# Second half's row variances moved from VectorE to ScalarE in a cross-attention and gated FFN kernel, with three groups of sums replanned

## The chip, the cores and the metric

The kernel runs on one core of one Trainium2 chip. The metric is device time in microseconds (us) of one execution; the median of three runs before the change is 1160.4 (1158.4 to 1164.2). Engines are called as in the profile: PE is TensorE (matmuls and transposes), PEld its weight loads, DVE is VectorE, ACT is ScalarE, POOL is GpSimd, and SP is SyncE, which here only issues DMAs.

## The reference

Everything is float32. `x` and `ctx` are 16 sequences of 128 tokens of 1024 numbers.

```python
def _layernorm(x, axis=-1, eps=1e-05):
    m = jnp.mean(x, axis=axis, keepdims=True)
    v = jnp.var(x, axis=axis, keepdims=True)
    return (x - m) / jnp.sqrt(v + eps)
...
query = q @ w_q.T          # q = _layernorm(x); 32 heads of 32
key = k @ w_k.T            # k = v = ctx; 8 groups of 32
value = v @ w_v.T
scores = jnp.einsum('bghnd,bgsd->bghns', query, key) / D_HEAD ** 0.5
scores = jnp.where(mask, scores, jnp.finfo(scores.dtype).min)
attention = jax.nn.softmax(scores, axis=-1)
out = jnp.einsum('bghns,bgsd->bghnd', attention, value)
...
x = x + out @ w_out.T
x12 = jnp.einsum('bsk,mk->bsm', _layernorm(x), w12) + b12
x1, x2 = jnp.split(x12, 2, axis=-1)
x = x + jnp.einsum('bsm,nm->bsn', jax.nn.silu(x1) * x2, w3) + b3
```

The first layernorm is what the change concerns. Its mean is taken out of the weights of the query product ahead of time (`centre`, L442), so that the product runs on the raw `x`. Its standard deviation comes in later: the scores are multiplied by the row's 1/std when they are masked (L760). So the variance of a token is needed only once attention reaches that token's sequence.

## The kernel before, in words

**Halves.** The 2048 tokens are two halves T = 0 and 1 of eight sequences (`NT` = 8). Sequence t belongs to half t // 8. The tile `mr[T]` holds two numbers for each token of a half: in row 0 the mean (or minus it), in row 1 the variance, which `inv_std` (L213) turns into 1/std with five small POOL instructions and two of ACT (Ln, Exp).

**Products by seven.** Large matrix products are not done with eight block products but with seven, as in Strassen's method: sums and differences of blocks of the left and right operand are made first ("left sums", "right sums"), and each product's result is added into several outputs. `seven` (L272) runs one such group; the order of the seven products is a tuple like (1, 5, 6, 7, 2, 3, 4). In the query stage a product is four matmuls of 512 columns, and steps 0 to 9 take them in the order (1, 5, 6, 7, 2, 3, 4). After each product it calls `hook(j)`, j = 1 to 7, through which all other work is placed.

**The query stage.** The query product uses seven twice, one inside the other. The outer level has products 1 to 7 ("outer 7"), the inner level too. A *step* is one outer product for one half g of the output rows: `Q_STEPS` has 14 of them, outer 1, 2, 6, 7, 4, 5, 3 in this order, each for g = 0 and 1. So steps 6 and 7 are outer 7, and steps 12 and 13 are outer 3. Each step has seven inner products of its own, and four sums of right-hand blocks (inner sums 5, 6, 7, 4 in the code's numbering) that both steps of an outer product share. `q_outer_right` (L488) makes the outer blocks, most of them on POOL; `q_inner_right` (L501) makes the inner sums, all on DVE.

The plan is written by hand: `q_at(n, j, fn, ...)` (L472) puts a call at hook j of step n, and `q_plans` (L633) holds the table. In the tables `((5, 2), (5, 7), (6, 1), (6, 2))` for outer 7 means: inner sum 5 is issued at hook 2 of step 5, sum 6 at hook 7 of step 5, sum 7 at hook 1 of step 6, sum 4 at hook 2 of step 6. Calls at one place run in the order in which they were registered.

**Order of instructions.** PE follows the source order throughout, and DVE from the start to the end of the first half's attention. In steps 0 to 9 (`AHEAD` = 10) ACT, POOL and SP follow it too. Elsewhere a scheduler orders ACT, POOL and SP by priority and by when memory is free. An engine waits at the head of its own queue: what stands behind a waiting instruction waits as well.

**Memory.** Nearly all operands of 128 x 1024 live in one pool of `NUNIT` = 44 units, 4 KB for each partition. A load or a sum that needs a new unit waits until one has had its last reader. PSUM has eight banks.

**Variances.** For the first half, tile t (128 tokens x 1024) is loaded by SP at hook 1 of step t + 1 (`load_xs`, L416), and `q_squares` (L622) runs at hook 2 of step t + 2, on ACT: one pass that sums the row, one tiny instruction that makes it minus the mean, and one pass that sums the squares of the centred row. For the second half, the loads are issued in the keys' and values' second round (`seven_round(1, k)`, L716; hooks 1 to 4 of each k), and `q_stats` (L617) runs at hooks 3 to 6: `mean_var` (L205), that is two BATCH_NORM_STATS2, an aggregate and a copy on DVE. The last one is followed by `inv_std`.

**After step 9.** Attention of the first half begins. It is cut into 16 units (a sequence and half of its heads); PE's other work is cut into the units by a cost: steps 10 to 13, then the rounds (1, 0) and (1, 1) for the second half's keys and values, then the first round of the output product. A unit takes DVE four times an instruction that scales and masks the scores (`s`, L760) and a row maximum (`nmax`, L763); ACT takes the exponentials (`p`, L769); DVE inverts the sums (`inv`, L778); POOL multiplies (`p`, L781); PE transposes (`pt`, L788); DVE and ACT copy the result out of PSUM (`pT`, L791 and L793); and PE multiplies by the values (`o`, L803). In the rounds (1, k) DVE and POOL also make the right sums of the context (`ctx_T`, `ctx`, L700) and of the output weights (`wo_T`, `wo`, L242), and POOL makes the left sums of the keys' weights (`sums_left7`, tile `A_S`, L303).

Of the kernel before, what the change touches and what calls it, by code (L numbers as in the profile page):

```python
# [13 lines left out]
AF = mybir.ActivationFunctionType  # L14
ALU = mybir.AluOpType
# [5 lines left out]
D = 1024  # L21
# [10 lines left out]
NT = B // 2  # L32
# [96 lines left out]
def xattn_ffn_kernel(  # L129
# [33 lines left out]
    nc = tc.nc  # L163
# [11 lines left out]
    def temp(shape, name):  # L175
        return temps.tile([P, *shape], F32, tag="tmp", name=name)
# [14 lines left out]
    def load(src, shape, name, eng=nc.sync):  # L191
        t = unit(shape, name)
        eng.dma_start(t, src)
        return t
# [10 lines left out]
    def mean_var(xt, dst, name):  # L205
        st = small.tile([P, 2, nc.vector.BN_STATS_DIM], F32, tag="st", name=f"st_{name}")
        for h in range(2):
            nc.vector.bn_stats(st[:, h, :], xt[:, ts(h, 512)])  # L208
        mv = small.tile([P, 2], F32, tag="mv", name=f"mv_{name}")
        nc.vector.bn_aggr(mv, st)  # L210
        nc.vector.tensor_copy(dst, mv)

    def inv_std(mr, name):  # L213

        n = mr.shape[2]
        v, t = (small.tile([P, NT], F32, tag=f"inv_std{i}", name=f"is{i}_{name}", bufs=2)[:, :n] for i in range(2))
        y = mr[:, 1, :]
        nc.gpsimd.tensor_scalar(v, y, EPS, None, ALU.add)
        nc.scalar.activation(t, v, AF.Ln)
        nc.scalar.activation(y, t, AF.Exp, scale=-0.5)  # L220
        nc.gpsimd.tensor_mul(t, y, y)
        nc.gpsimd.tensor_mul(t, t, v)
        nc.gpsimd.tensor_scalar(t, t, -0.5, 1.5, ALU.mult, ALU.add)
        nc.gpsimd.tensor_mul(y, y, t)
# [177 lines left out]
    mr = [const.tile([P, 2, NT], F32, tag=f"mr{T}", name=f"mr_{T}") for T in range(2)]  # L402
    later, xs = [], {}

    def soon(n, gen):

        later.append([n, gen])

    def tick():
        for item in list(later):  # L410
            item[0] -= 1
            if item[0] <= 0:
                later.remove(item)
                stream.work.appendleft(item[1])

    def load_xs(t):  # L416
        xs[t] = load(x[t], [D], f"xs_{t}")

    def stats(t):
        mean_var(xs.pop(t), mr[t // NT][:, :, t % NT], f"a{t}")  # L420

    def turn_V(T, c, r, t):

        pt = bank(f"vt_{T}_{c}_{r}").rearrange("p (t k) -> p t k", t=4)
        for i in range(4):
            nc.tensor.transpose(pt[:, i, :], t[:, ts(i, S)], ident)
            yield 0.17
        if (T, c) not in V:
            V[T, c] = unit([4, KV], f"V_{T}_{c}")
        nc.scalar.copy(V[T, c][:, :, ts(r, P)], pt)  # L430

    def key_home(T, c, r):
        if (T, c) not in KT:
            KT[T, c] = unit([GH, 512], f"K_{T}_{c}")
        return KT[T, c][:, r, :]
# [36 lines left out]
    def q_at(n, j, fn, *args):  # L472
        qplan.setdefault((n, j), []).append((fn, args))
# [140 lines left out]
            *((INNER,) if n < AHEAD else ((1, 6, 5, 7, 2, 3, 4), nc.vector.tensor_copy)),  # L614
        )

    def q_stats(t):  # L617
        stats(t)
        if t % NT == NT - 1:
            inv_std(mr[t // NT], f"a{t // NT}")  # L620

    def q_squares(t):  # L622

        xt = xs.pop(t)
        less = mr[0][:, 0, t : t + 1]
        nc.scalar.activation(xt, xt, AF.Identity, accum_out=less)
        nc.scalar.mul(less, less, -1.0 / D)
        nc.scalar.activation(xt, xt, AF.Square, bias=less, accum_out=mr[0][:, 1, t : t + 1])
        if t == NT - 1:
            nc.gpsimd.tensor_scalar(mr[0][:, 1, :], mr[0][:, 1, :], 1.0 / D, None, ALU.mult)  # L630
            inv_std(mr[0], "a0")

    def q_plans():  # L633
        for n, (g, i) in enumerate(Q_STEPS):
            if i > 2:
                q_at(n - 2, 3, q_load_left, g, i)
            for e, k in enumerate((1, 5, 6, 7, 3)):
                q_at(n - 1, 3 + e if n else min(5 + e // 2, 7), q_inner_left, g, i, k)
            if i in (1, 2, 5, 3):
                q_at(n - 1, 6 if n else 7, q_hold, g, i)  # L640
            if i == 1:
                q_at(g - 1, 7, q_keep_left, g, 4)
                q_at(g - 1, 7, q_outer_left, g)
                q_at(g, 7, q_keep_left, g, 3, 6)
                q_at(g + 1, 2, q_keep_left, g, 5, 7)
                q_at(n + 1, 2, q_store, g, i, "U")
            if i == 2:
                q_at(n + 1, 2, q_gather, g, 2, "U")
                q_at(n + 2, 3, q_final, g, 2, 0, 0)
            if i == 6:  # L650
                q_at(n - 2, 4, q_fetch, g, "U")
                q_at(n + 1, 2, q_store, g, "u", "V")
            if i == 7:
                q_at(n + 1, 2, q_store, g, "u", "W")
            if i == 4:
                q_at(n, 7, q_stay, g, "u", 1)
            if i == 5:
                q_at(n + 1, 3, q_gather, g, "V", 5)
                q_at(n + 1, 3, q_gather, g, "W", 5)
                q_at(n + 1, 4, q_given, g, "W", 1)  # L660
            if i == 3:
                q_at(*((n + 1, 3) if g == 0 else (n, 7)), q_gather, g, "V", 3)
                q_at(n, 7, q_given, g, "V", 0)
        for e, (K, C) in enumerate(((0, 0), (1, 0), (1, 1), (0, 1))):
            for f, (h, c) in enumerate(((0, 0), (0, 1), (1, 1), (1, 0))):
                when = ((-1, 3 + (f + 1) // 2), (0, 1 + f), (0, 5 + f // 2), (1, 2 + f))[e]
                q_at(*when, load_xq, K, C, h, c)
        for i, hcs, ks in (
            (1, [(-1, 5)] * 4, ((-1, 6), (-1, 6), (-1, 7), (0, 1))),
            (2, [(0, 6)] * 4, ((0, 7), (1, 1), (1, 2), (1, 7))),  # L670
            (5, [(2, 1), (2, 2), (2, 7), (3, 1)], ((8, 7), (9, 1), (9, 2), (9, 7))),
            (6, [(2, 7), (3, 1), (3, 3), (3, 3)], ((3, 5), (3, 6), (3, 7), (4, 1))),
            (7, [(4, 5), (5, 1), (5, 2), (5, 5)], ((5, 2), (5, 7), (6, 1), (6, 2))),
            (4, [(6, 5), (7, 1), (7, 2), (7, 5)], ((7, 2), (7, 7), (8, 1), (8, 2))),
            (3, [(4, 4)] * 4, ((4, 4), (5, 4), (8, 4), (8, 6))),
        ):
            for when, hc in zip(hcs, ((0, 0), (0, 1), (1, 1), (1, 0))):
                q_at(*when, q_outer_right, i, *hc)
            for when, k in zip(ks, (5, 6, 7, 4)):
                q_at(*when, q_inner_right, i, k)  # L680
        for t in range(NT):
            q_at(t + 1, 1, load_xs, t)
            q_at(t + 2, 2, q_squares, t)
        for m in (0, 1, 4, 5):
            q_at(8, 1 + m, q_home, 0, m)
        q_at(11, 3, load_left7, 1)
        for j, e in ((1, 0), (1, 5), (2, 1), (4, 3)):
            q_at(12, j, lambda e=e: ctx_work[1][e][1]())
        for when, i, e in (
            ((12, 6), 5, 0), ((12, 7), 5, 1), ((13, 2), 6, 0), ((13, 4), 6, 1), ((13, 5), 7, 0), ((13, 7), 7, 1),  # L690
        ):
            q_at(*when, ctx_sum, i, e)
        q_at(13, 3, sums_left7, 1, 0)

    def ctx_sum(i, e):

        R, (a, b) = ctx_R[1], {5: (0, 1), 6: (3, 5), 7: (3, 0), 4: (2, 6)}[i]
        if e == 0:
            R[i] = R[0] if i == 7 else [unit([2, 512], f"ctx_1_T{i}_{h}") for h in range(2)]
        (nc.vector if i in (5, 6) else nc.gpsimd).tensor_sub(R[i][e], R[a][e], R[b][e])  # L700
# [15 lines left out]
    def seven_round(T, k, R):  # L716
        def done(rc, s, ps):
            r, c = rc
            dst = temp([512], f"vT_{T}_{c}_{r}") if k else key_home(T, c, r)
            if s is None:  # L720
                nc.scalar.copy(dst, ps)
            else:
                nc.vector.tensor_add(dst, s, ps)
            if k:
                soon(3, turn_V(T, c, r, dst))

        def hook(j):
            tick()
            if (T, k, j) == (1, 0, 4):
                sums_left7(1, 1)  # L730
            if (T, k) == (1, 0) and j < 3:
                ctx_sum(4, j - 1)
            if T == 1 and j < 5:
                load_xs(NT + 4 * k + j - 1)
            if T == 1 and j > 2 and j < 7:
                q_stats(NT + 4 * k + j - 3)
            transition(T, k, j)

        yield from seven(left7.pop((T, k)), R, f"Q7_{T}_{k}", done, hook, (1, 2, 5, 6, 7, 3, 4))
# [616 lines left out]
    for t in range(8, B):  # L1356
        n, j = divmod(t - 8, 2)
# [68 lines left out]
```

## Time and profile before

| | us |
|---|---|
| median of three runs (lowest, highest) | 1160.4 (1158.4, 1164.2) |
| the profiled execution | 1160.87 |
| its span, first to last instruction | 1159.1 |

| stage (us from the span's start) | length | PE | DVE | ACT | POOL |
|---|---|---|---|---|---|
| first keys and values, 0 to 57.7 | 57.7 | 55.9 | 27.8 | 12.5 | 33.2 |
| query steps 0 to 9, 57.7 to 181.3 | 123.6 | 121.6 | 103.3 | 31.8 | 89.5 |
| first half's attention, 181.3 to 356 | 174.7 | 166.9 | 146.7 | 105.5 | 111.6 |
| second half's attention and output product, 356 to 600 | 244.0 | 242.3 | 177.7 | 153.0 | 141.0 |
| rest of it and FFN's first product, 600 to 976 | 376.0 | 374.8 | 255.2 | 61.3 | 167.0 |
| FFN's second product, 976 to 1159.1 | 183.1 | 179.0 | 138.7 | 31.5 | 103.5 |

The columns under the engines are busy time in us. A line of the timeline gives the start, the duration, the engine, the source line, the operation and its operands as "output <- inputs", and in brackets the idle time before it with what ended it. The name of a tile is without its number: `Y_T` is an inner right sum of the query stage, `xq` a block of `x`, `Q_b` a PSUM bank of a query step (the keys' and values' rounds use the same name), `QI` an inner left sum, `QL` a left operand fetched again, `xs` a tile of `x` for the variances, `st_a` the statistics of DVE.

Steps 0 to 9 begin at 57.7, 71.0, 83.0, 95.0, 107.0, 119.0, 131.1, 145.3, 157.3 and 169.3, so a step takes 12.0, but for step 0 (13.3) and step 6 (14.2). Steps 10 to 13, between units of attention, begin at 182.5, 196.8, 214.0 and 233.5; the round (1, 0) begins at 258.7.

### The profile page before, as it was taken

What the parts mean: (1) busy time and instruction counts of PE and PEld (TensorE: products, weight loads), DVE (VectorE), ACT (ScalarE), POOL (GpSimd) and SP (SyncE); (2) the same over time, 40 slices, a digit from 0 to 9 for tenths busy, and PEclk for the clock granted to TensorE, in tenths of its full rate; (3) what the DMA queues carried; (4) which work ended last, traced back from release to release, by engine and by line L of the source; (5) the groups of instructions that cost most, each with busy time, mean ns of one, the idle gap of its engine ahead of it and who ended that gap; (6) DMA issues with size and microseconds to landing.
All of it is one profiled execution on the core that took longest, in us unless ns stands there. A gap on an engine that the chain in (4) does not pass through costs nothing.

```text
span 1159.1 us, 13631 instructions
## 1 busy us (share of the span) xinstructions
PE 1140.4 (98%) x4232; PEld 533.0 (46%) x4232; DVE 849.4 (73%) x1179; ACT 395.6 (34%) x1429; POOL 645.7 (56%) x591
## 2 busy tenths in 40 slices
PE   9999999989999999999999999999999999999998
PEld 4444444544544455444454544444444444444443
DVE  4577988798897778778545456757777887979872
ACT  1222234556666576676361321110011022111211
POOL 5669935776468556646533359822523342548455
PEclk9999999999999999999999999999999999999999
DMA  9699675955344330332584889758734878272411
GB/s 365 254 372 346 223 267 150 214 134 180 110 164 183 128 128 37 128 128 110 182 308 163 333 327 327 228 199 264 171 130 157 214 192 270 91 268 86 172 74 72
DMA packets 70232, 227.42 MB, mean 196 GB/s; under 512 B 7824, under 2 KB 7824, under 8 KB 70160
## 3 DMA queue, kind: packets, MB, share of 16 engines
q1 hardware_dynamic: 62672, 199.81, 46.4%
q0 software_dynamic: 6624, 24.12, 11.2%
q10 hardware_dynamic: 864, 2.62, 0.6%
q8 instruction: 34, 0.56, 0.2%
q14 instruction: 38, 0.31, 0.1%
HBM read 139.49 MB, written 79.69 MB: 189 GB/s over the span
## 4 chain that ended last, share of the span: by engine, by line
PE 70%; DVE 4%; ACT 1%; issue 1%; POOL 1%; DMA 0%; SPq 0%; POOLq 0%; DVEq 0%; ACTq 0%
PE F_b L199 28%; PE G_b L199 15%; PE O_b L199 15%; PE pt L788 3%; PE Q_b L199 3%; PE s L751 2%; PE o L803 2%; DVE s L760 1%; PE xt L903 1%; DVE nmax L763 1%; ACT p L769 0%; DMA xnr<-xn_dram 0%; POOL p L781 0%; DVE xnT L1079 0%; DVE st_a L208 0%
## 5 line engine op out<-in xcount | busy, mean ns | idle before, releaser
L769 ACT ACTIVATE p<-s,nmax 128x128 f32<-128x128 f32 x512 | 181.5, 402 | 117.7 <-DVE nmax L763 102.8
L781 POOL TENSOR_TENSOR p<-p,inv 128x512 f32<-128x512 f32 x128 | 132.2, 1067 | 124.9 <-DVE inv L778 105.2
L199 PE MATMUL F_b<-X_T,L 128*128 128x512 f32 x304 | 135.7, 592 | 0.0
L769 ACT ACTIVATION_READ_ACCUMULATOR p<-s,nmax 128x1 f32 x512 | 123.2, 241 | 0.0
L760 DVE SCALAR_TENSOR_TENSOR s<-s,mr,drop 128x512 f32<-128x512 f32 x128 | 93.0, 749 | 36.2 <-PE s L751 36.1
L199 PE MATMUL G_b<-w_R,A_L 128*128 128x512 f32 x256 | 114.7, 592 | 0.0
L788 PEld LDWEIGHTS pt<-ident,p 128*128 128x128 f32 x512 | 63.0, 141 | 70.4 <-issue 59.7
L199 PEld LDWEIGHTS F_b<-X_T,L 128*128 128x128 f32 x304 | 57.4, 190 | 70.8 <-issue 69.1
L763 DVE TENSOR_REDUCE nmax<-s 128x4 f32<-128x512 f32 x128 | 85.1, 685 | 2.2
L284 ACT COPY F_p<-F_b 128x512 f32<-128x512 f32 x28 | 16.4, 586 | 188.3 <-PE F_b L199 188.3
L303 POOL TENSOR_TENSOR x<-x,G_n 128x512 f32<-128x512 f32 x36 | 52.6, 1487 | 49.6 <-DVE G_n L366 32.6
L788 PE MATMUL pt<-ident,p 128*128 128x128 f32 x512 | 76.9, 273 | 2.5 <-POOL p L781 1.4
L384 ACT COPY G_c<-G_b 128x512 f32<-128x512 f32 x52 | 30.5, 586 | 140.8 <-PE G_b L199 140.7
L199 PEld LDWEIGHTS G_b<-w_R,A_L 128*128 128x128 f32 x256 | 48.6, 190 | 61.5 <-issue 58.8
L1189 DVE TENSOR_TENSOR M<-F_u,F_b 128x512 f32<-128x512 f32 x57 | 39.0, 685 | 47.2 <-PE F_b L199 43.4
L303 POOL TENSOR_TENSOR x<-x,G_c 128x512 f32<-128x512 f32 x36 | 51.4, 1447 | 32.3 <-DMA x<-x_dram 13.2
L199 PE MATMUL Q_b<-Y_T,QI 128*128 128x512 f32 x136 | 62.5, 595 | 2.3 <-DVE Y_T L509 2.0
L199 PE MATMUL O_b<-wo_T,O_S 128*128 128x512 f32 x128 | 63.3, 603 | 0.0
L199 PE MATMUL O_b<-wo,O_S 128*128 128x512 f32 x128 | 62.5, 602 | 0.0
L199 PE MATMUL F_b<-xnT,L 128*128 128x512 f32 x128 | 60.9, 593 | 0.0
L199 PE MATMUL O_b<-wo,OTr 128*128 128x512 f32 x112 | 56.1, 604 | 0.5 <-ACT p L769 0.5
L287 DVE TENSOR_TENSOR F_u<-F_b,F_p 128x512 f32<-128x512 f32 x28 | 19.3, 690 | 44.9 <-PE F_b L199 41.2
(244 smaller groups left out, 2259.1 us busy)
## 6 DMA issues: line engine op xcount, KB each, us to landing
w<-in_w_dram SPq DMA_DIRECT2D x36, 512.0 KB, 6.4
xq<-in_xT_dram SPq DMA_DIRECT2D x16, 512.0 KB, 9.5
xs<-in_x_dram SPq DMA_DIRECT2D x16, 512.0 KB, 5.8
xp<-in_x_dram SPq DMA_DIRECT2D x16, 512.0 KB, 6.6
x_dram<-xp SPq DMA_DIRECT2D x16, 512.0 KB, 2.8
xn_dram<-xn SPq DMA_DIRECT2D x16, 512.0 KB, 2.9
xnr<-xn_dram SPq DMA_DIRECT2D x16, 512.0 KB, 6.0
h<-hT_dram SPq DMA_DIRECT2D x16, 512.0 KB, 5.9
```

The costliest lines, as they stand in the source:

```text
L199: nc.tensor.matmul(ps, lhsT, rhs, start=start and i == 0, stop=stop and i == len(pairs) - 1, skip_group_check=True,)
L287: nc.vector.tensor_add(u1, banks[6], p1)
L303: (eng.tensor_add if op == "+" else eng.tensor_sub)(out, a, b)
L384: nc.scalar.copy(t, ps)
L751: nc.tensor.matmul(ps[gl][:, j, :], QT[T, gh * HPG + j][rows, c, toks], KT[T, c][rows, gh, toks], start=True, stop=True,)
L760: nc.vector.scalar_tensor_tensor(s, s, rstd, drop.unsqueeze(1).to_broadcast([P, HPG, S]), ALU.mult, ALU.add,)
L763: nc.vector.tensor_reduce(nmax[e], s, AX.X, ALU.max, negate=True)
L769: nc.scalar.activation(p[:, j, :], ps[gl][:, j, :], AF.Exp, bias=nmax[e][:, j : j + 1], accum_out=total[:, e, j : j + 1],)
L781: nc.gpsimd.tensor_mul(p, p, inv[:, e].unsqueeze(2).to_broadcast([P, HPG, S]))
L788: nc.tensor.transpose(pt[:, j, :], p[:, j, :], ident)
L803: nc.tensor.matmul(o[ds(gl * DH, DH), :, :], V[T, c][:, i, ts(gh * GL + gl, DH)], pTs[gl], start=True, stop=True,)
L1189: nc.vector.tensor_add(dst, s, ps)
```

## The change

The helpers `stats` and `q_stats` go, and with them the loads and the statistics in the second round. `q_squares` is generalised to both halves, and the second half's tiles are loaded and squared in steps 3 to 7, two in each step. Besides, five places in the table change: outer 7's inner sum 6 goes from (5, 7) to (5, 4); outer 3's inner sums 6, 7 and 4 go from (5, 4), (8, 4), (8, 6) to (8, 3), (8, 5), (9, 4); and the left sums of the keys' second round go from (13, 3) to (12, 2).

```diff
-    def stats(t):
-        mean_var(xs.pop(t), mr[t // NT][:, :, t % NT], f"a{t}")
-
...
-    def q_stats(t):
-        stats(t)
-        if t % NT == NT - 1:
-            inv_std(mr[t // NT], f"a{t // NT}")
-
     def q_squares(t):
 
         xt = xs.pop(t)
-        less = mr[0][:, 0, t : t + 1]
+        T, e = divmod(t, NT)
+        less = mr[T][:, 0, e : e + 1]
         nc.scalar.activation(xt, xt, AF.Identity, accum_out=less)
         nc.scalar.mul(less, less, -1.0 / D)
-        nc.scalar.activation(xt, xt, AF.Square, bias=less, accum_out=mr[0][:, 1, t : t + 1])
-        if t == NT - 1:
-            nc.gpsimd.tensor_scalar(mr[0][:, 1, :], mr[0][:, 1, :], 1.0 / D, None, ALU.mult)
-            inv_std(mr[0], "a0")
+        nc.scalar.activation(xt, xt, AF.Square, bias=less, accum_out=mr[T][:, 1, e : e + 1])
+        if e == NT - 1:
+            nc.gpsimd.tensor_scalar(mr[T][:, 1, :], mr[T][:, 1, :], 1.0 / D, None, ALU.mult)
+            inv_std(mr[T], f"a{T}")
...
-            (7, [(4, 5), (5, 1), (5, 2), (5, 5)], ((5, 2), (5, 7), (6, 1), (6, 2))),
+            (7, [(4, 5), (5, 1), (5, 2), (5, 5)], ((5, 2), (5, 4), (6, 1), (6, 2))),
             (4, [(6, 5), (7, 1), (7, 2), (7, 5)], ((7, 2), (7, 7), (8, 1), (8, 2))),
-            (3, [(4, 4)] * 4, ((4, 4), (5, 4), (8, 4), (8, 6))),
+            (3, [(4, 4)] * 4, ((4, 4), (8, 3), (8, 5), (9, 4))),
...
         for t in range(NT):
             q_at(t + 1, 1, load_xs, t)
             q_at(t + 2, 2, q_squares, t)
+            q_at(3 + t // 2, 3 + t % 2 * 2, load_xs, NT + t)
+            q_at(4 + t // 2, 4 + t % 2 * 2, q_squares, NT + t)
...
-        q_at(13, 3, sums_left7, 1, 0)
+        q_at(12, 2, sums_left7, 1, 0)
...
-            if T == 1 and j < 5:
-                load_xs(NT + 4 * k + j - 1)
-            if T == 1 and j > 2 and j < 7:
-                q_stats(NT + 4 * k + j - 3)
             transition(T, k, j)
```

## The prediction

> **What bounds the kernel now.** I read the page first, then who waited for whom on PE, then the chain of waits of the two stretches that the diff touches, then the timelines of PE, DVE, POOL and SP there.
>
> ```profile
> span 1159.1 us, 13631 instructions
> PE 1140.4 (98%) x4232; PEld 533.0 (46%) x4232; DVE 849.4 (73%) x1179; ACT 395.6 (34%) x1429; POOL 645.7 (56%) x591
> ```
>
> PE sets the time. An edit on another engine is worth only the holes that it closes in PE's row, or opens. The waits of PE (total us, times, longest) name them; of these the change can reach four:
>
> ```profile
> PE Q_b L199 <- DVE Q_u L290: 2.0, 1, 2.0
> PE Q_b L199 <- DVE Y_T L509: 2.0, 1, 2.0
> PE s L751 <- DVE pT L793: 1.6, 2, 0.9
> PE pt L788 <- POOL p L781: 1.4, 1, 1.4
> ```
>
> Matmuls overlap, so this view understates a hole. I size holes on PE's timeline: start to start, less the usual 0.43 us for a matmul of 512 columns and 0.11 for a transpose. That gives three places: **136.6** (2.1 us, query step 6), **242 to 254** (7.3 us, step 13) and **321 to 352** (1.2 + 0.9 + 0.8 + 1.5 = 4.4 us, the keys' and values' second round). Closing all is worth 13.8 us, 1.2%: no gain can be larger.
>
> **Part A, sums of outer 7 and outer 3.** PE's matmuls, and DVE before them:
>
> ```profile
> 127.50 1.74 DVE L509 TENSOR_TENSOR Y_T<-xq,Y_T 128x1024 f32<-128x1024 f32 x1
> ...
> 133.10 3.37 DVE L509 TENSOR_TENSOR Y_T<-xq,Y_T 128x1024 f32<-128x1024 f32 x1
> ```
> ```profile
> 132.77 1.88 PE L199 MATMUL Q_b<-Y_T,QI 128*128 128x512 f32 x4
> 136.61 1.96 PE L199 MATMUL Q_b<-Y_T,QI 128*128 128x512 f32 x4 [1.96 <-DVE Y_T L509]
> ```
>
> The product at 136.61 is the third of step 6, and the sum at 133.10 is its operand (outer 7, sum 6, planned at (5, 7)). The sum at 127.50 is outer 3's sum 6, planned at (5, 4), read by no product before step 12. The diff gives that place to outer 7. Its block (1, 1) comes from POOL at 121.27 (the pair of 6.10 us from 115.16), in time for 127.50. The hole of 2.1 goes. Next late is sum 7, which moves up to 133.1: if POOL slows it as it slowed the sum now there, it ends at 133.10 + 3.37 = 136.47, and PE, 1.72 per product from 131.06, wants it at 136.21. That leaves 0.3. Value: **gain 1.9**, bounds 0 to 2.1.
>
> Outer 3's sums land in steps 8 and 9. Step 8 keeps its count. Step 9 gets one more, 1.21 us as at 169.12; DVE is busy 10.76 of 12.30 us from 169.0 to 181.3, so 1.5 of idle time covers it. Without this cover it would lengthen the hole at 190.29, where PE waits 0.8 for DVE's Q_p. Value 0, bounds -1.2 to 0.
>
> **Part B, no statistics in the second round.** Each of the eight tiles costs DVE two BATCH_NORM_STATS2 of 0.68, an aggregate of 0.21 and a copy of 0.17: 1.7, together 13.6 us. Until 311 PE has no hole for them. After it, they lie on the chain of waits (start, us, what):
>
> ```profile
> 313.92 1.21 DVE st_a L208 x2
> ...
> 325.48 1.20 DVE st_a L208 x2
> ...
> 328.97 1.21 DVE st_a L208 x2
> ...
> 339.11 1.21 DVE st_a L208 x2
> ...
> 340.85 0.10 POOL is_a L218
> ...
> 350.90 1.05 POOL p L781
> ```
>
> From 307 to 341 this chain is DVE without a break (31.03 busy of 32 us from 311 to 343); from start to next piece the four take 1.61 + 1.64 + 1.65 + 1.74 = 6.6. Then it passes to POOL, which sat idle 3.19 before 340.85 for the last variance and worked off O_S and wo_T late, so that p at 350.90 held PE's transposes. With 6.6 less on the chain, the scores set its start. First hole: DVE's s begins at 318.49 and could not begin before PE's scores end at 318.0, so 0.5 of 1.2 goes. Second and third (337.9, 339.3) wait for banks that ACT's p frees after DVE's nmax; two more statistics (3.3), less 1.4 in which DVE would then wait for PE's products, make that 1.9 earlier, so they go: 0.9 + 0.8. Fourth: POOL no longer waits and drops five small instructions; its two wo_T and two O_S (7.3 us) end before inv, so 1.5 goes. Value: **gain 3.7**, bounds 0 (the same holes return with wo_T or ACT as releaser) to 4.4.
>
> **Part C, what the query stage takes on.** ACT: a tile's squares run from 133.45 to 136.12, 2.67 us; two more per step in steps 4 to 7 are 5.3. Queued behind them is the copy of Q_p; it sits idle 8.88 before its product in these steps, so 3.5 of cover is left. Value 0. The row says that the work is dearer on ACT, 2.67 against 1.7 on DVE.
>
> The Trainium skill ("ScalarE: Activation LUTs", Rules for kernel authors) speaks against this move: adds and multiplies belong on VectorE. Its figure for a pointer bias, 280 ns + 0.833 ns per element, would give 1.13 per pass as an estimate, beside the 1.15 measured; by the rule the move would be a loss of a microsecond per tile, if ACT were the bound.
>
> POOL at (7, 6) waits for the last square before the inverse roots. By ACT's rows that is near 154, with one left sum of step 8 behind it, read by PE after 163. Value 0.
>
> SP: eight loads of 512 KB move up from the second round. DMA share is 1.05 from 94 to 106, 1.03 from 106 to 119, then 0.71. Four loads fall in the full stretches: 2.1 MB at some 330 GB/s, 6.4 us for whatever lands behind them. First to feel it is step 6's left operand: issued 109.44, landed 119.56, read by POOL at 121.23, 1.7 of margin. POOL is nearly full from there to 155; its lateness next meets DVE at 147.19, where outer 4's sum needs the block done at 142.02. That margin of 5.2 shrinks by A's 2.1, so PE pays beyond 1.7 + 3.1 = 4.8. Value 0 (the loads are spread over 25 us and SP sits idle between 95.4 and 102.1 and between 112.4 and 121.8), bounds -1.6 to 0.
>
> **Part D, keys' left sums at (12, 2).** Eight POOL instructions, 246.40 to 254.9 with two p between, move before POOL's difference of the context. The DVE sum beside them took 3.30 from 244.22: POOL's context sum ends at 246.43, and 246.43 + 1.21 is 247.64, about the 247.52 measured. So that sum, not the left sums, held DVE; the first pair of left sums took 2.38 instead of the later 1.42. Moving them saves DVE nothing there, and PE's 2.0 at 253.81 hangs on DVE's Q_u behind four pairs of s and nmax. Value 0; bounds -1 (p behind 5.9 us of sums at the new place) to +5.8, the first rival.
>
> **The sum.** 1.9 + 3.7 = 5.6 from the profiled execution's 1160.87 (span 1159.1 and 1.8 around it): 1155.3. The median of the runs is 1160.4, 0.5 lower, so **1154.8**. A and B at their upper ends give 1153.9; A at 0 and C at -1.6 give 1158.3: the forecast's own range.
>
> **Rivals.** *1, the clock hole closes too.* At 238.61 a DVE context sum takes 3.23 instead of 1.22, beside POOL's from 238.18. PE's scores then wait (2.1), and the clock drops:
>
> ```profile
> 245.00:249.00 4.00, 4.00 (x12) 0.57 0.06 11
> ```
>
> The columns are PE busy, granted clock, DMA share, GB/s. 4.0 x (1 - 0.57) = 1.7 is lost by the clock. If the left sums fill POOL's idle 4.55 before 237.47 and push its context sum behind DVE's, 2.1 + 1.7 go, and up to the 2.0 at 253.81: 3.8 to 5.8. Time 1149 to 1151. Against it: nothing makes POOL's sum wait if the left sums run at the idle 221 to 226. Chance 0.22.
>
> *2, the second round keeps its holes* (B at 0, with wo_T and p as the new releasers): 1160.4 - 1.9 = 1158.5. For it: DVE still has 4.6 us of wo_T there. Chance 0.12.
>
> *3, the pool of 44 units runs out* (slower). Counted from first write to last read in source order, 41 units are live in step 4; the change adds up to three x tiles there, 44. SP takes loads in order and already waited 6.7 once for a unit before 102.07. If the left operands of steps 6 and 7 sit behind x tiles that wait for a unit, the wait is in steps of 12.04, since squares run at fixed places. PE pays what exceeds 4.8. One step: 12.04 - 4.8 = 7.2 above the forecast, 1162 (chance 0.06, within 0.5%). Two steps: 19.3, 1174 (chance 0.15). It makes the kernel slower by over 0.5% once the operands are 4.8 + 5.6 + 5.8 = 16.2 late. Against it: SP has 9.4 idle before 121.8 in which to catch up.
>
> **How the numbers follow.** The forecast has 0.45. Runs here scatter so that 0.5% (5.8 us: below 1154.6 or above 1166.2) is about what can be told from no change; the forecast sits on that edge, so half of it counts as faster. Faster: 0.225 + 0.22, 0.45. Same: 0.225 + 0.12 + 0.06, 0.40. Slower: 0.15. The range runs from rival 1's lower end, with a microsecond for scatter, over the forecast, rival 2 and one step of rival 3, with the edge of it: 1148 to 1166.
>
> **What would show it.** A: step 6 without an idle entry ahead of its third product. B: no st_a in the second round, DVE with idle time between 311 and 343, PE's four holes gone or with other releasers. C: ACT idle some 3.5 before Q_p in steps 5 to 8; left operands landed before POOL reads them. D: PE's clock between steps 13's products. I would be wrong if SP's issues in steps 3 to 6 come later than their readers, or if DVE's freed time leaves the holes with POOL.

## The result, and the profile after

The changed kernel takes 1164.85 us (median of 20 runs, 1161.99 to 1166.88) where the kernel before takes 1160.93 (20 runs, 1158.41 to 1164.21): ratio 1.003, 95% interval 1.0021 to 1.0038. It is slower by 0.3%, where the forecast was 5.6 us less. The time lies inside the range of 1148 to 1166, but above the time before, where the forecast lay below it. The profiled execution took 1164.01.

The page after, to be held against the two lines shown of before:

```profile
span 1162.2 us, 13637 instructions
PE 1142.4 (98%) x4232; PEld 533.3 (46%) x4232; DVE 841.8 (72%) x1147; ACT 415.4 (36%) x1469; POOL 650.3 (56%) x592
```

The work moved as the diff says: DVE has 32 instructions fewer, ACT 40 more. The 32 instructions took 13.9 in all, yet DVE's busy time falls by 7.6 only, as other sums on it take longer (those into `QUr` 3.5 in all, those into `A_L` 2.7; why is not shown). The span grew by 3.1. The waits of PE (total us, times, longest) have a new line at the top; the 1.4 of `pt` for POOL's `p` is down to 0.3, and the 2.0 for `Y_T` to 0.3:

```profile
PE Q_b L199 <- POOL QI L303: 4.4, 2, 4.1
PE Q_b L199 <- DVE Q_u L290: 2.0, 1, 2.0
PE s L742 <- DVE pT L784: 1.6, 2, 0.9
PE Q_b L199 <- DVE Q_p L284: 1.4, 1, 1.4
...
PE Q_b L199 <- DVE xq L506: 1.1, 1, 1.1
...
PE pt L779 <- POOL p L772: 0.3, 1, 0.3
PE Q_b L199 <- DVE Y_T L506: 0.3, 1, 0.3
```

Where the time went is read from the starts of the steps (line numbers after are up to 9 lower than before):

| us | before | after | difference (from unrounded times) |
|---|---|---|---|
| up to step 5 | 119.0 | 118.8 | -0.2 |
| step 5 | 12.0 | 18.6 | +6.6 |
| step 6 | 14.2 | 13.4 | -0.9 |
| steps 7 to 12 | 88.3 | 89.5 | +1.2 |
| step 13 | 25.1 | 25.2 | 0.0 |
| start of round (1, 0) to the end | 900.4 | 896.8 | -3.6 |

So the second round gave what was hoped for, and step 5, which no step of the prediction had touched, took it back and more. **What happened in step 5** begins on POOL. Its timeline after, and then before (start, duration, what, in brackets the idle time before it and what ended it):

```profile
108.01 0.86 POOL L570 DMA_DIRECT2D QM<-QU_dram  x1 [0.63 <-DVE QM L603]
119.46 0.72 POOL L303 TENSOR_TENSOR QI<-QL 128x256 f32<-128x256 f32 x1 [10.59 <-DMA Q_dram<-QM]
...
121.28 2.36 POOL L496 TENSOR_TENSOR xq<-xq,xq 128x1024 f32<-128x1024 f32 x1
...
124.97 4.66 POOL L496 TENSOR_TENSOR xq<-xq,xq 128x1024 f32<-128x1024 f32 x2
...
131.37 0.73 POOL L303 TENSOR_TENSOR QI<-QI,QL 128x256 f32<-128x256 f32 x1
```
```profile
108.23 0.86 POOL L573 DMA_DIRECT2D QM<-QU_dram  x1 [0.62 <-DVE QM L606]
108.79 1.05 POOL L303 TENSOR_TENSOR QI<-QL 128x256 f32<-128x256 f32 x1
```

The same left sum, the first of step 5, started at 108.79 and now starts at 119.46. Its input was there: the `QL` that it reads had landed at 102.80. What it lacked was a place for its output: it is the first writer of a new unit of the pool. Before, the only wait in front of it is for PE, so the unit came from an operand that PE had read; with the x tiles live in steps 3 to 7 the next free one is a `QM` tile, which is held until SP's store to `Q_dram` has landed. That store was issued 2.2 late, because SP, in order, was itself waiting for a unit for an x tile (the second `xs` of the first line is issued at 106.99, after a wait that a matmul of PE ended). SP after, and then before:

```profile
99.87 7.46 SPq L193 DMA_DIRECT2D xs<-in_x_dram  x2
107.43 1.57 SPq L577 DMA_DIRECT2D Q_dram<-QM  x2
```
```profile
102.07 0.33 SPq L193 DMA_DIRECT2D xs<-in_x_dram  x1
105.27 4.05 SPq L580 DMA_DIRECT2D Q_dram<-QM  x2
```

It landed at 119.30, 11.9 after its issue; before, it was issued at 105.27 and landed at 112.92. POOL, then 10.6 late, holds DVE and PE. DVE's row after, then PE's after, then PE's before for the same products:

```profile
127.36 3.35 DVE L506 TENSOR_TENSOR Y_T<-xq,xq 128x1024 f32<-128x1024 f32 x1 [6.63 <-POOL xq L496]
```
```profile
126.21 1.88 PE L199 MATMUL Q_b<-Y,QL 128*128 128x512 f32 x4
132.19 3.54 PE L199 MATMUL Q_b<-Y,QI 128*128 128x512 f32 x4 [4.10 <-POOL QI L303]
135.52 2.03 PE L199 MATMUL Q_b<-Y_T,QL 128*128 128x512 f32 x4
```
```profile
125.91 1.88 PE L199 MATMUL Q_b<-Y,QL 128*128 128x512 f32 x4
127.62 1.88 PE L199 MATMUL Q_b<-Y,QI 128*128 128x512 f32 x4
129.34 1.88 PE L199 MATMUL Q_b<-Y_T,QL 128*128 128x512 f32 x4
```

PE waits for the sum that POOL ends at 132.10, the left operand of step 5's sixth product. Behind the hole the same four matmuls take 3.54 instead of 1.88: the granted clock is down to about a half (0.55 from 132.1 to 135.5). Hole (4.3), an earlier one at 124.39 (0.4) and the slow matmuls (1.8) make 6.5 of the 6.6. Later, 1.3 is lost at 143.80, where DVE is still behind. Of the 1.2 in steps 7 to 12, 0.5 lie in step 8 and 0.7 in step 10.

### The profile page after: what moved, and what is told of

Read it like the earlier page. It is cut to its first block, busy times and chain, and to the rows that moved or that the text cites. A ratio compares the mean times of both kernels' runs of the same rounds, so it can differ in the third digit from the quotient of the medians.

```text
span 1162.2 us, 13637 instructions
## 1 busy us (share of the span) xinstructions
PE 1142.4 (98%) x4232; PEld 533.3 (46%) x4232; DVE 841.8 (72%) x1147; ACT 415.4 (36%) x1469; POOL 650.3 (56%) x592
## 4 chain that ended last, share of the span: by engine, by line
PE 72%; DVE 2%; ACT 1%; issue 1%; DMA 0%; POOL 0%; SPq 0%; ACTq 0%; DVEq 0%; POOLq 0%
PE F_b L199 28%; PE G_b L199 15%; PE O_b L199 15%; PE Q_b L199 4%; PE pt L779 4%; PE s L742 2%; PE o L794 2%; PE xt L894 1%; ACT p L760 1%; DVE s L751 1%; DVE xnT L1070 0%; DVE nmax L754 0%; DMA xnr<-xn_dram 0%; ACT xn L868 0%; POOL p L772 0%
## 5 line engine op out<-in xcount | busy, mean ns | idle before, releaser
L784 DVE COPY pT<-pt 128x512 f32<-128x512 f32 x64 | 42.8, 670 | 13.6 <-PE pt L779 12.3
```

Source lines behind the costliest of these rows:

```text
L784: nc.vector.tensor_copy(pT, pt)
```

## The experiments

Each ratio is against runs of the kernel before on the same chip, between those of the experiment (its medians: 1160.25 for e1 to e4, 1161.21 for e5 to e8, 1160.82 for e9 and e10, 1161.28 for e11 and e12). Theory U: the wait is for a unit. Its rivals are T, the traffic of the loads, and S or A, the new places of the sums. "Later" kernels have the second half's loads and squares two steps later than the change.

**e1, the sums alone.** The kernel before with the new places of the outer 7 and outer 3 sums, nothing else.

```diff
-            (7, [(4, 5), (5, 1), (5, 2), (5, 5)], ((5, 2), (5, 7), (6, 1), (6, 2))),
+            (7, [(4, 5), (5, 1), (5, 2), (5, 5)], ((5, 2), (5, 4), (6, 1), (6, 2))),
...
-            (3, [(4, 4)] * 4, ((4, 4), (5, 4), (8, 4), (8, 6))),
+            (3, [(4, 4)] * 4, ((4, 4), (8, 3), (8, 5), (9, 4))),
```

> The kernel before with only the new places of outer 7's and outer 3's sums; second half's variances stay on DVE in the second round, keys' left sums at (13, 3). Theory U (units: the x tiles take the free units in steps 3 and 4, so that POOL's left sums of step 5 get a unit that is free only when a store of a query block has landed, 10.6 us of idle POOL): no x tile is added, so no such wait; POOL starts step 5's left sums near 108.8, the hole of 2.1 ahead of step 6's third product goes, and the time is 1.5 to 2.1 below before, 1159. Theory T (the added loads' traffic delays all that lands from 94 to 131): the same 1159. Theory S (the new places of the sums are what costs, since DVE waits at (5, 4) or (5, 2) for POOL's block): the hole near 132 is there, and the time is 3 to 7 above before.

1161.18, ratio 0.9997 (0.9986 to 1.0008). No hole in step 5, so the sums do not cause it. The hole in step 6 fell from 2.1 to 0.4, and that step from 14.2 to 12.5. But nothing arrives at the end: step 13 took 28.2 instead of 25.1. A hole of 1.1 at 249.09 is new there, the one near 252 waits 2.5 instead of 2.0, and the clock takes more: 0.94, 0.50 and 0.71 in the three stretches of 4 us from 248, which is 3.4 us lost, where before had 0.68 and 0.89 from 244, 1.7. So the time fits none of the three forecasts; what speaks against S is the trace.

**e2, no variances.** The changed kernel without the second half's loads and variances (set to 1), so that part of the computation is left out.

```diff
+    nc.vector.memset(mr[1], 1.0)
...
-            q_at(3 + t // 2, 3 + t % 2 * 2, load_xs, NT + t)
-            q_at(4 + t // 2, 4 + t % 2 * 2, q_squares, NT + t)
```

> The changed kernel without the second half's variances: its eight loads and squares are left out, and 1 stands in place of 1/std for that half. All else as changed. Theory U and theory T: no hole in step 5; the 1.9 of step 6 and the 3.0 that the second round gave in the changed kernel's trace are both won: 1156 (5 below before). Theory S: the hole near 132 is there, 1161 to 1163.

1156.62, ratio 0.9956 (0.9941 to 0.9971). Steps 5 and 6 take 12.0 each. The loads or the squares are the cause.

**e3, two steps later.**

```diff
-            q_at(3 + t // 2, 3 + t % 2 * 2, load_xs, NT + t)
-            q_at(4 + t // 2, 4 + t % 2 * 2, q_squares, NT + t)
+            q_at(5 + t // 2, 3 + t % 2 * 2, load_xs, NT + t)
+            q_at(6 + t // 2, 4 + t % 2 * 2, q_squares, NT + t)
```

> The changed kernel with the second half's loads and squares two steps later (loads in steps 5 to 8, squares in steps 6 to 9), past the steps in which most units are live. Theory U: step 5's left sums on POOL follow the POOL work before them without a wait for a landing, no hole near 132, the second round keeps its 3.0: 1156 to 1157. Theory T: the loads now lie where the DMA share is 0.45 to 0.9, so part of the hole goes: 1156 to 1160. Theory S: 1163 to 1165.

1156.66, ratio 0.9954 (0.9941 to 0.9968), faster than both kernels, with all of the change's work in it. Step 5's first left sum runs at 108.34 without a wait; steps 5 and 6 take 12.0 and 12.4. It is the place of the loads, not their number.

**e4, 46 units.** The changed kernel, all traffic at the change's places, with `NUNIT` 46 instead of 44 and, to make room, 10 instead of 14 of the temporaries.

```diff
-NUNIT = 44
-NTMP = 14
+NUNIT = 46
+NTMP = 10
```

> The changed kernel with 46 units of 4 KB in place of 44, paid for with 10 temporaries of 2 KB in place of 14; every load at the changed kernel's place. Theory U: POOL starts step 5's left sums by 112 (119.5 in the changed kernel), and the hole of 4.3 ahead of step 5's third last product is under 0.5; the whole time may lose some of it again to the fewer temporaries in attention, 1156 to 1162. Theory T: traffic is unchanged, so POOL's start stays later than 116 and the hole is 3 to 4.5.

1162.34, ratio 1.0008 (0.9995 to 1.002). The hole in step 5 is gone: steps 5 and 6 take 12.0 each with the loads where the change has them. POOL's row:

```profile
108.94 1.05 POOL L303 TENSOR_TENSOR QI<-QL 128x256 f32<-128x256 f32 x1
```

The store of the first product landed as late as 119.87 here, and POOL did not wait for it. That is U. The time comes back elsewhere: attention has larger holes than in e3 (start to start 2.2 at 323.28, where e3 has 1.0, and 1.4 at 349.13). That the fewer temporaries make them is likely but was not tried alone, so the total says nothing of U.

**e5, the old sums.** The changed kernel with the sums of outer 7 and outer 3 at their old places (e1's diff, undone).

> The changed kernel with Part A undone: outer 7's second sum back at (5,7), outer 3's sums back at (5,4), (8,4), (8,6); the second half's loads and variances and the keys' left sums stay where the change puts them. Theory U (the loads' units make POOL's left sums of step 5 wait for the store of the first product): the wait needs only the loads, so it stays. POOL stands idle some 10 us ahead of step 5's left sums, PE has a hole of about 4 us near 132 and, since outer 7's sums stand as before, a hole of about 2 us more in step 6; step 5 takes 16 to 19 us. Time 1163 to 1168 where the kernel before takes 1160.3. Theory A (the moved sum on DVE, together with the loads, makes the hole): no hole near 132, steps 5 and 6 as before, and the second round's gain stays: 1156 to 1158.

1168.68, ratio 1.0073 (1.0057 to 1.009): U, 0.7 over its range. Step 5 takes 18.6 as in the changed kernel, step 6 16.6. Part A had hidden 3.2 of what the wait does to step 6.

**e6, later with the old sums**: e3 without Part A (e1's diff, undone).

> The kernel with the second half's loads and variances two steps later (1156.66 where before took 1160.25), with Part A undone in it: what A is worth beside B. Prediction's Part A: the hole of 2.1 ahead of step 6's third product is back and costs 1.7 to 1.9 at the end too: 1158.4. Rival (given back, as the sums alone showed): step 6 loses 1.7 more, and step 13 loses about that much less, so 1156 to 1157 and no difference that can be measured.

1159.83, ratio 0.9983 (0.9969 to 0.9997). Step 6 has its hole back (1.5) and takes 13.7 instead of e3's 12.4, so A is worth 1.2 there. The profile's step 13 also lost 1.3 more than e3's, with the clock at 0.50 over 4 us and more. Its runs fall in two groups: three at a mean clock of 0.999 (1154.7 to 1156.6), nine at 0.996 or 0.997 (1159.1 to 1160.8). Which of the two an execution gets decides 4 us; A's share in that is not settled.

**e7, later with the keys' left sums at their old place**: e3 without Part D.

```diff
-        q_at(12, 2, sums_left7, 1, 0)
+        q_at(13, 3, sums_left7, 1, 0)
```

> The same kernel (1156.66 where before took 1160.25) with Part D undone alone: the keys' left sums, k = 0, back at (13,3). Prediction's Part D: nothing, 1156 to 1157.5, and only POOL's order in steps 12 and 13 differs. Rival: the eight sums (about 5.8 us of POOL) stand behind the context sums and the numerators at (13,3), so that the second round starts late: up to 5.8 more, at most 1162.5; or their place at (12,2) has cost something in step 12: 1155.

1157.49, ratio 0.9964 (0.9952 to 0.9976), beside 0.9954 with it: no difference that can be told.

**e8, POOL's context sums later in the source**, in e3.

```diff
-... ((13, 4), 6, 1), ((13, 5), 7, 0), ((13, 7), 7, 1),
+... ((13, 4), 6, 1),
...
-            if (T, k) == (1, 0) and j < 3:
-                ctx_sum(4, j - 1)
+            if (T, k) == (1, 0) and j < 5:
+                ctx_sum(7 if j < 3 else 4, (j - 1) % 2)
```

> The same kernel (1156.66 where before took 1160.25) with the four context sums that POOL makes (outer 7's and outer 4's) one round later: outer 7's ahead of the second round's products 1 and 2, outer 4's ahead of products 3 and 4. In all kernels so far DVE's context sums of step 13 take 3.2 to 3.3 us instead of 1.2 while one of POOL's runs beside them, and step 13 has holes of 0.9, 0.7, 1.1 and 2.6 us and then 4 to 6 us at half clock. Theory P (the sums slow each other): DVE's take 1.2 each, the holes shrink to 1 to 2 in all, and with a hole too short to open the clock's gate the half clock goes: 1151 to 1154. Rival (DVE has too much to do there whatever POOL does): the second hole stays at over 1.5 and the half clock with it: 1155 to 1157. A second rival: the sums come too late for the second round's fifth and seventh products: a new hole between 262 and 275, 1157 to 1160.

1154.83, ratio 0.9955 (0.9939 to 0.997). It says nothing of theory P. Behind step 9 POOL does not follow the source: its two sums of outer 7 ran at 235.53 and 241.45, as before, and only those of outer 4 moved. DVE's still took 3.2 and 3.3.

**e9, DVE's context sums set apart**, in e3:

```diff
-            ((12, 6), 5, 0), ((12, 7), 5, 1), ((13, 2), 6, 0), ((13, 4), 6, 1), ((13, 5), 7, 0), ((13, 7), 7, 1),
+            ((12, 6), 5, 0), ((13, 1), 5, 1), ((13, 3), 6, 0), ((13, 4), 6, 1), ((13, 5), 7, 0), ((13, 7), 7, 1),
```

> The kernel with the second half's loads and variances two steps later (1156.66 where before took 1160.25), with two of DVE's four context sums of step 13 set apart from POOL's: outer 5's second from (12,7) to (13,1), outer 6's first from (13,2) to (13,3). Each of POOL's two waits for the sum of DVE's that reads the same tile, so it starts right after it and lies beside DVE's next one, which takes 3.2 to 3.3 us instead of 1.2. Theory P (the sums of the two engines slow each other where they lie side by side): all four take about 1.2, DVE wins some 4 us in step 13, the holes of 1.1, 1.0 (near 241) and 1.1, 2.6 (near 250) shrink by 3 to 5 in all, step 13 takes 22 to 24 us instead of 26.7: 1152 to 1154. Rival (the order of the work sets the holes, not DVE's time): the holes move and keep their sum, step 13 takes 26 to 27: 1156 to 1157. If the holes go and 3 to 6 us of half clock stay, the clock's gate is set by something else than these holes: 1154 to 1156.

1154.36, ratio 0.9938 (0.9925 to 0.9951). Step 13 takes 25.1. Both sums of outer 6 now take 1.2. Outer 5's second one took 3.94: it lies beside the end of POOL's sum and beside the two numerators that POOL multiplies after it. The holes became one of 3.06, and the half clock stayed.

**e10, the traffic alone.** The changed kernel with SP copying the second half's x tiles from memory to memory at the change's places, and the variances left out (set to 1).

```diff
+    def move_xs(t):
+        nc.sync.dma_start(tc.dram_tile([P, D], F32, name=f"xs_dram_{t}"), x[t])
...
-            q_at(3 + t // 2, 3 + t % 2 * 2, load_xs, NT + t)
-            q_at(4 + t // 2, 4 + t % 2 * 2, q_squares, NT + t)
+            q_at(3 + t // 2, 3 + t % 2 * 2, move_xs, NT + t)
```

> The changed kernel with the second half's tiles of x copied from memory to memory by SP at the places where the change loads them, so that the traffic stays and no unit of the pool is taken; the second half's variances are left out (set to 1), so the output is not the reference's in that half. Theory U (units): POOL's left sums of step 5 start without a wait near 108, no hole near 132, steps 5 and 6 take 12.0 to 12.5 each; time as with loads and variances left out, 1156 to 1158 (1156.62 where before took 1160.25). Theory T (traffic delays the store that frees the unit, and other landings): the store of the first product lands 9 us or more after its issue instead of 7.65 as in the kernel before, a hole of over 2 us comes back in step 5 or 6: 1160 to 1164.

1157.17, ratio 0.9965 (0.9952 to 0.9978): U. The store flew even longer, from 105.98 to 119.59, and POOL did not care, as no output of its own hung on it. POOL's row:

```profile
108.06 0.86 POOL L574 DMA_DIRECT2D QM<-QU_dram  x1 [0.62 <-DVE QM L607]
108.63 1.05 POOL L303 TENSOR_TENSOR QI<-QL 128x256 f32<-128x256 f32 x1
```

Traffic makes the store late (13.6 instead of 7.6 us); the missing unit makes that lateness PE's. The store's late issue in the changed kernel was not what counted: here and in e4 it was issued on time (105.98 and 105.76) and landed just as late.

**e11, behind the copies**: e9 with outer 5's second sum at (13,2) instead of (13,1).

> The kernel with the second half's loads and variances two steps later and the context sums set apart, with outer 5's second sum at (13,2) instead of (13,1), so that on DVE it stands behind the two copies that PE waits for (with it at (13,1): 1154.36 where before took 1160.82; that sum took 3.94 beside POOL's sum and numerators and made a hole of 3.06 at 242.5, followed by half clock from 242 to 249, worth 2.8 more; step 13 took 25.0). Theory G (a hole of about 2 us or more in a busy PE sets half clock behind it): the hole goes, and with it the half clock, step 13 takes 19 to 20.5: 1148.5 to 1150.5. Rival (half clock comes in this step whatever the holes): the hole goes, step 13 takes 21.5 to 22.5: 1151 to 1152. Second rival (the sum now delays the scores' arithmetic behind it, and the hole moves to the tile's transposes near 245): 1153 to 1155.

1152.93, ratio 0.9926 (0.991 to 0.9943): the fastest version, under both kernels. Step 13 takes 23.1. The hole at 242.5 is gone, and so is the half clock behind it. But a hole of 2.6 is back at 247.46, at DVE's `Q_u` behind four pairs of `s` and `nmax`, with half clock behind it: near to the second rival, whose hole was to lie elsewhere and whose time was to be 1153 or more.

**e12, the same sums in the kernel before**, nothing of the change.

> The kernel before with the same two places of context sums alone (outer 5's second sum at (13,2), outer 6's first at (13,3)), nothing of the change in it. It tells what step 13 is worth without the change. If the step's holes and the half clock behind them are independent of the change: step 13 takes 19 to 20.5 instead of 25.1, so 4.5 to 6 less than before: 1154.5 to 1156.5, with the holes of the second round and of step 6 as in before. If the gain is given back later, as the sums of outer 7 alone were: 1158.5 to 1161.

1156.72, ratio 0.9957 (0.994 to 0.9973). Step 13 takes 21.4 instead of 25.1: a gain of its own, with nothing to do with the variances, and a little under what was expected because the last hole stays.

## Why the prediction was wrong

**Part C failed: "Value 0 (the loads are spread over 25 us and SP sits idle ...), bounds -1.6 to 0."** It measured what loads can do by the bytes that land ahead of others, and looked at the left operands. Those cost nothing: the one for step 6 landed at 121.78 in the changed kernel, before POOL was ready for it, and in e4, where POOL was on time, at 122.35; there POOL waited 1.05 for it and PE not at all. The runs put in its place: loads hold units, and the first to lack one was POOL, for an output, while the last holder of the freed unit was a store in flight. Cost: 6.6 in step 5. Shown by e3 (place), e4 (units) and e10 (traffic without units). The idle time of SP, which was to absorb the loads, was no slack either: before, it is 6.7 of waiting for a unit until 102.07 and 9.3 of waiting for DVE until 121.84, and what stands behind in SP's queue waits too. Another value of 0 in Part C was nearly right: POOL waited for the last square until 160.99, where the text had 154, and PE lost 0.4 at 166.62 soon after; whether the one made the other was not tried.

**Rival 3 had the cause and not the path.** It counted 44 live units of 44, and the runs fit that count: with 44 and the loads at the change's places POOL had to wait, with 46 (e4) it did not. It then let the shortage act only through SP's loads, in steps of 12.04, against 4.8 of cover, and gave one such step 1162. A count equal to the size should have led to the question for each engine that writes a new unit near that place: who held the unit last, and how is it released? Here the unit freed by PE's reading came on time; the one that hung on a store's landing came 11.9 us after the store's issue (7.6 to 14.1 in the traces of before, e3, e4 and e10 for the same store).

**Part A, gain 1.9 (0 to 2.1): the mechanism was right.** The hole fell to 0.4 in e1, where the text left 0.3, and in e6 against e3 the step differs by 1.2. In the changed kernel it shows only as 3.2 saved of a larger loss (e5: 16.6 against 13.4). What the sum left out is that e1's 1.7 did not reach the end; why is not settled (see the last section). Outer 3's sums at their new places cost at most 0.7 at the hole that was at 190.29 (1.5 instead of 0.8), inside the bounds, and nothing in e3 (0.8).

**Part B, gain 3.7 (0 to 4.4): right, and some 3.0 in size.** From the start of round (1, 0) to the end the changed kernel won 3.6, but before had a hole of 1.15 at 591.35, at a load, of which the changed kernel has only 0.4. e3 and e6 to e9, which have that hole, won 2.8 to 3.1 from there to the FFN's first product. That is what PE's timeline says: two of the four holes are left, 0.95 and 0.46 by start to start, where it had 1.2, 0.9, 0.8 and 1.5, so 3.0 of 4.4 went. (The 1.2, the 0.8 and the 0.95 are whole distances from start to start; less the usual, they are 1.1, 0.7 and 0.8, and 2.9 of 4.2 went. At the second hole, 337.93, the profile names POOL's O_S as releaser, and not ACT, so the reason that the text gave for it is not shown.) The mis-sized terms are the first hole (0.25 instead of 0.5) and the fourth (1.1 instead of 1.5):

```profile
328.11 0.66 PE L423 MATMUL vt<-ident,vT 128*128 128x128 f32 x4 [0.37 <-ACT p L760]
357.00 0.66 PE L779 MATMUL pt<-ident,p 128*128 128x128 f32 x4 [0.29 <-POOL p L772]
```

On the chain of waits DVE's stretch now ends at 326; between 328 and 356 the chain is PE's. DVE's first `s` follows PE's scores (DVE idle 3.30 before 313.73, released by `s` of L742):

```profile
312.61 1.14 PE s L742 x32
313.75 0.75 DVE s L751
...
328.11 0.66 PE vt L423 x4
328.76 0.86 PE Q_b L199 x2
```

At the fourth hole POOL's `p` is still the releaser.

**Part D, 0: right** (e7).

**Rival 1** hoped that D would set POOL's and DVE's sums apart. It didn't: nothing makes POOL's sum wait, as the text itself said. Setting DVE's sums apart from POOL's by hand gave 5.0 in e12 (by its ratio), inside its 3.8 to 5.8, and 3.3 in e11 against e3, below it.

**The sum.** A and B were to bring 5.6; step 5's 6.6, 1.0 less from step 6 than hoped and 1.2 in steps 7 to 12 turned -5.6 into +3.1 in the profiled spans, but for 0.1. With the loads two steps later (e3) the forecast's number nearly comes out: 0.9954 of before, against 1154.8 of 1160.4, which is 0.9952. That agreement is partly luck, for e3's step 13 loses 1.5 more than before's, and its profiled span is only 3.6 shorter. The ceiling of 13.8 was about 1 too high: without its last hole e12's row from the scores at 239.35 to the product at 248.26 takes 6.3, and before took 12.6 for the same work, so step 13's place was worth 6.3 and not 7.3. Nothing else in the text rests on it.

## What to carry to other kernels

Before a load is moved earlier, count the live units there, and if the count reaches the size of the pool, ask for every engine that opens a unit nearby who freed it last: here the answer was a store's landing, and that put a delay of the DMA queues into POOL's row and then into PE's. The cure may be free: the same loads two steps later gained 0.5% where the change lost 0.3%. And a hole that is closed need not shorten the kernel by its length: in e1 the 1.7 won in step 6 did not show at the end, where step 13 took 3.0 more.

## What the runs showed of the hardware

**A sum of two tiles in SBUF (the engines' working memory) on DVE stands still while POOL reads there.** A context sum of 128 x 1024 on DVE takes 1.22 alone. e3's timeline of DVE, then of POOL:

```profile
234.65 1.22 DVE L695 TENSOR_TENSOR ctx_T<-ctx,ctx 128x1024 f32<-128x1024 f32 x1
...
236.38 3.23 DVE L695 TENSOR_TENSOR ctx_T<-ctx,ctx 128x1024 f32<-128x1024 f32 x1
...
242.00 3.31 DVE L695 TENSOR_TENSOR ctx_T<-ctx,ctx_T 128x1024 f32<-128x1024 f32 x1
```
```profile
235.96 2.56 POOL L695 TENSOR_TENSOR ctx<-ctx,ctx 128x1024 f32<-128x1024 f32 x1
...
241.88 2.34 POOL L695 TENSOR_TENSOR ctx<-ctx,ctx 128x1024 f32<-128x1024 f32 x1
```

The slow ones end at 239.61 and 245.31, each 1.09 after POOL's instruction (238.52 and 244.22). In e9 and e11 the sum that lay beside POOL's numerators ended 1.10 after the last of these (240.75 and 240.08). So the sum does not run slowly beside POOL; it takes its time as if it started when POOL is through, even past three of POOL's instructions in a row. The Trainium skill says this ("SBUF — State Buffer", Who interferes with whom): a DVE instruction with two inputs in SBUF and a GpSimd instruction that reads SBUF exclude each other for the whole instruction. The four cases agree. DVE's copies and reductions from PSUM beside the same POOL instructions kept their 0.64 to 0.69.

**The same hole, two clocks.** e11 and e12 have the same hole ahead of the same product (PE's timeline, one line of each), and then different clocks. First e11, then e12, each with its window from 248 to 252 (the columns are the length, the busy time of PE, PEld, DVE, ACT and POOL, the granted clock, DMA share and GB/s):

```profile
247.46 1.79 PE L199 MATMUL Q_b<-xq,QI 128*128 128x512 f32 x2 [2.48 <-DVE Q_u L290]
```
```profile
248.00:252.00 4.00, 4.00 (x13) 2.24 (x12) 2.94 (x5) 2.00 (x8) 1.47 (x2) 0.60 0.08 30
```
```profile
248.26 1.13 PE L199 MATMUL Q_b<-xq,QI 128*128 128x512 f32 x2 [2.48 <-DVE Q_u L290]
```
```profile
248.00:252.00 4.00, 3.74 (x16) 2.15 (x17) 4.00 (x7) 2.71 (x12) 4.00 (x4) 1.00 1.00 343
```

0.60 over 4 us is 1.6 us of work lost, 1.00 nothing. A hole of this size thus had two prices. So had a pair of holes ahead of the scores in step 13: before waits 0.88 and 0.71 there, until 243.75, and has a clock of 0.68 from 244 to 248; e1 has the same two waits, until 242.13, and a clock of 1.00 from 240 to 248.

The times of the kernel before go with the clock as well: of its 69 runs beside the experiments, 30 had a mean clock of 0.998 or more (median 1159.5) and 39 less (median 1162.6). Where the clock fell in these runs is not recorded. The Trainium skill ("TensorE: Matmul & The Clock Gate", Part 1) says that the clock is halved after an idle window of about 3.4 us, and that these windows run freely and do not start with the kernel. No run here shows the windows. The holes of 2.5 in e1 and e11 are shorter than such a window, and half clock followed them all the same, so the length alone does not settle it; that the place of a hole in a window decides is a guess that no run here tries.

What stays open is why step 13 takes 3.0 more in e1 than in before. Before pays for its clock behind the pair and then waits 2.0 at the last hole; e1 pays nothing behind the pair, comes to its last holes sooner, waits 1.0 and 2.5 there, and pays behind the last. Whether the length of that hole or its moment decided was not tried.
